# A clock model in the planner, spare products in planned gaps, and a new order of preference for a two-layer kernel

## The chip, the core and the metric

The kernel runs on one core of a Trainium2 chip. A core has a matrix engine (TensorE, PE in the profile, with its weight loads as PEld), a vector engine (VectorE, DVE), a scalar engine (ScalarE, ACT), a general engine (GpSimd, POOL) and a queue engine that issues DMAs (SyncE, SP). The metric is the device time of one launch in microseconds, the median over several runs. The profile is one execution taken by the hardware profiler; its span runs from the first to the last instruction.

## The reference

The input x is 8 sequences of 512 tokens with 256 channels, in float32. Two layers follow each other; after each of the four blocks comes x = layernorm(x + block(x)).

1. **Retention.** q, k, v = x W_qkv, 16 heads of 16 channels. ret = (q k^T) with a causal decay per head; r = ret v + (q past_kv) x 256; then a normalization over a whole sequence (mean and variance of all heads, tokens and channels), with a weight and a bias per head.
2. **Feed-forward with ternary weights.** W_fc (1024 x 256) and W_proj (256 x 1024) are quantized to -1, 0, 1 by thresholds at half of their mean magnitude. h = layernorm(gelu(x W_fc^T)), then the product with W_proj.
3. **Attention within a token.** An RMS norm, q, k, v for 16 heads of 16 channels, elu on q and k, and for each token a product over its heads, in two halves whose difference is taken with a factor lambda; RMS norms over a head and over the token; then two 256 x 256 products with a gelu between, and a residual.
4. **Routed experts.** Tokens in 2 groups of 2048, a router to 8 experts, two per token, at most 160 tokens per expert and group. Each expert computes relu(x wi) wo with 1024 hidden channels; results are summed with the gates.

## The kernel before

All work is cut into stages, one per sequence b (batch) or expert i, each written as a Python generator. `stage_a1` is retention (transposes of x, projections, then four chunks of 128 tokens: scores `sc`, masking into `scm`, values `r_ps`, a running state). `stage_a2` is its normalization and residual (two tiny products `gn_ps`, `gn_ps2`, then transposes `r_tp`). `stage_b` is the feed-forward (transposes, `fc_ps`, gelu and squares, `pr_ps`). `stage_bn` is the layer norm behind it, on VectorE, GpSimd and ScalarE alone. `stage_c1` is the attention of block 3 (transposes of x, `qk_ps`, `v_ps`, then per chunk `v_tp`, `hs`, masking into `hm`, `at_ps`). `stage_c2` is all behind that: the RMS norms on VectorE, transposes of a, the products `w1_ps` and `w2_ps`, the layer norm, its stores (`x3_d`, `y_d`), and the router's logits. `choose` and `route` select experts and build the lists of rows. `gather`, `dispatch`, `expert_in`, `expert_out` and `combine` do the experts, and `finish` the last layer norm. `prepare_ffn` and `prepare_l1` quantize or transpose the weights once.

The order of instructions on every engine is made by a planner when the program is built. `op` places an operation off TensorE on a model of its engine, with a cost in us, and puts it into a list by planned start; `pe(cost)` advances the planned time of TensorE, `Plan.now`. A stage yields when it would wait: `need(t)` for data and a free PSUM bank, `hold` for a buffer, `later` for time alone. `bank` hands out one of eight PSUM banks, the one released first, and `release` gives it back at a planned time. `interleave` (L250) holds a list of streams. Each turn it asks every stream when its next stage could go on, and takes the earliest; TensorE work can't go before `Plan.now`, so several streams often have equal times, and then the one that stands first in the list wins:

```python
                if on_pe:
                    t = max(t, Plan.now)
                if best is None or t < best[0]:
                    best = t, i
```

Each engine executes its instructions in the order that results, waiting where a semaphore says so. The planner's costs thus decide only the order; what a wait really takes is decided on the chip. Lists of streams stand at the end of `tile_layers`: weights of the experts first, then loads of x, `c2`, `bn`, `c1`, gathers, dispatches, routing, `a2`, weights' preparation, `a1`, `b`, and the experts' stages.

PSUM results are moved off by ACT or DVE. In the profile nearly all instructions off TensorE carry line L204, since `op` issues them; they are told apart by the names of their tiles. A float32 product shows as two MATMUL rows, a transpose or a product in the rounded float32 format of `fc_ps` as one.

Of the kernel before, what the change touches and what calls it, by code (L numbers as in the profile page):

```python
# [21 lines left out]
B, S, D = 8, 512, 256  # L22
# [59 lines left out]
def tile_layers(ctx: ExitStack, tc: tile.TileContext, ins, out, at):  # L82
# [64 lines left out]

    class Plan:
        now = 0.0
        t = 0.0  # L150
        events = []
        count = 0
# [62 lines left out]

    def pe(cost):

        Plan.now = Plan.t = max(Plan.now, Plan.t) + cost
        return Plan.now + PE_OUT

    def bank(name):
# [28 lines left out]
    def interleave(streams):  # L250

        ends = {}
        queues = [list(q) for q in streams]
        at, kind = [0.0] * len(streams), ["other"] * len(streams)
        begun = [False] * len(streams)  # L260
        clock = 0.0
        first = {"a1", "b", "c1", "h", "e", "s", "d"}
        while any(queues):
            best = None
            for i, q in enumerate(queues):
                if not q:
                    continue
                key, deps, takes, _ = q[0]
                t = max(at[i], clock)
                on_pe = kind[i] == "pe"  # L270
                if not begun[i]:
                    if any(k not in ends for k in deps):
                        continue
                    if any(len(Plan.free[k]) < n for k, n in takes.items()):
                        continue
                    on_pe = key[0] in first
                    t = max([t] + [ends[k] + (HOP_PE if on_pe else 0.0) for k in deps])
                    t = max([t] + [sorted(Plan.free[k])[n - 1] for k, n in takes.items()])
                if on_pe:
                    t = max(t, Plan.now)  # L280
                if best is None or t < best[0]:
                    best = t, i
            t, i = best
            key, _, takes, gen = queues[i][0]
            if not begun[i]:
                begun[i] = True
                for k, n in takes.items():
                    take(k, n)
            clock = Plan.t = t
            flush(t)  # L290
            try:
                kind[i], at[i] = next(gen)
            except StopIteration as stop:
                ends[key] = max(t, stop.value or 0.0)
                queues[i].pop(0)
                begun[i], kind[i], at[i] = False, "other", t
        flush(HELD)
# [254 lines left out]
    with ExitStack() as stages:  # L552
# [253 lines left out]
        def load_x(b):  # L806
            if b > 0:
                fetch_x(b)
            t = Plan.t + (5.0 if b == 0 else 22.0 if b == 1 else 6.0)
            yield later(t)  # L810
            return t
# [177 lines left out]
        def stage_a2(b):  # L989

            rT, st, ready = rTs.pop(b)
            x_sb = xs[b]
            mv = wk.tile([P, 2], F32, tag="gn_mv", name=f"gn_mv_{b}")
            gs = wk.tile([P, 3], F32, tag="gn_s", name=f"gn_s_{b}")
            t = op(DVE, 0.26, ready, V.bn_aggr, mv, st)
            yield from need(t)
            ps = bank("gn_ps")
            T.matmul(ps[:, 0:1], ones, mv[:, 0:1], start=True, stop=True)

            def spread():  # L1000
                nc.vector.tensor_tensor(gs[:, 1:2], mv[:, 0:1], gs[:, 0:1], ALU.add)
                nc.vector.scalar_tensor_tensor(
                    gs[:, 1:2], gs[:, 1:2], gs[:, 1:2], mv[:, 1:2], ALU.mult, ALU.add
                )

            t = op(
                DVE, 0.15, pe(0.2), V.tensor_scalar, gs[:, 0:1], ps[:, 0:1], -1.0 / P, None, ALU.mult,
                bank=ps,
            )
            t = op(DVS, 0.42, t, spread)  # L1010
            yield from need(t)
            ps = bank("gn_ps2")
            T.matmul(ps[:, 0:1], ones, gs[:, 1:2], start=True, stop=True)
            t = rsqrt(gs[:, 2:3], ps[:, 0:1], 1.0 / P, LN_EPS, pe(0.2), bank=ps)

            ga = wk.tile([P, 2, 2], F32, tag="gn_a", name=f"gn_a_{b}")

            def affine():
                nc.vector.tensor_scalar(ga[:, 0, :], gnp[:, 0, :], gs[:, 2:3], None, ALU.mult)
                nc.vector.scalar_tensor_tensor(  # L1020
                    ga[:, 1, :], ga[:, 0, :], gs[:, 0:1], gnp[:, 1, :], ALU.mult, ALU.add
                )

            t = op(DVS, 0.48, t, affine)
            e1 = op(
                ACT, 0.81, t, A.activation, rT[:, 0, :], rT[:, 0, :], AF.Identity,
                bias=ga[:, 1, 0:1], scale=ga[:, 0, 0:1],
            )
            e2 = op(
                POOL, 0.76, t, GP.tensor_scalar, rT[:, 1, :], rT[:, 1, :], ga[:, 0, 1:2],  # L1030
                ga[:, 1, 1:2], ALU.mult, ALU.add,
            )
            r = x_sb
            ts = []
            for c2 in range(NC // 2):
                yield from need(max(e1, e2))
                ps = bank("r_tp")
                for c in range(2):
                    for m in range(2):
                        at_ = (c * 2 + m) * P  # L1040
                        c4 = c2 * 2 + c
                        T.transpose(ps[:, at_ : at_ + P], rT[:, m, c4 * P : (c4 + 1) * P], ident)
                e = op(
                    DVE, 0.68, pe(0.46), V.tensor_tensor,
                    r[:, c2 * 2 : c2 * 2 + 2, :].rearrange("p c d -> p (c d)"), ps,
                    x_sb[:, c2 * 2 : c2 * 2 + 2, :].rearrange("p c d -> p (c d)"), ALU.add, bank=ps,
                )
                ts += [e, e]
            give("aq", Plan.now)
            ends = layernorm(wk, r, r, ts, on_act=True)[3]  # L1050
            x1s[b] = r
            yield later(max(ends))
            return max(ends)
# [334 lines left out]
        def open_experts(k):  # L1388

            (ret_stack, ffn_stack)[k].close()  # L1390
            pools[k] = stages.enter_context(
                tc.tile_pool(name=f"mo{k}", bufs=1, side=("left", "right")[k], reuse_waits="tile")
            )
            yield later(Plan.t)
            return Plan.t
# [42 lines left out]
        def dispatch(g, pair):  # L1438

            rows, tag = gathered.pop((g, pair))  # L1440
            xsT[g, pair] = pools[0].tile(
                [P, NK, 2 * CAP], F32, tag="xsT", bufs=2, name=f"xsT_{g}_{pair}"
            )
            for k in range(NK):
                yield from need(0.0)
                ps = bank("xs_tp")
                for j, n in enumerate(COLS):
                    T.transpose(
                        ps[:, j * P : j * P + n], rows[:n, j, k * P : (k + 1) * P], ident[:n, :n]
                    )  # L1450
                done = op(
                    ACT, 0.43, pe(0.57), A.copy, xsT[g, pair][:, k, :], ps[:, : 2 * CAP], bank=ps
                )
            give(tag, Plan.now)
            yield later(done)
            return done
# [111 lines left out]
        def after(*keys):  # L1568
            return [k for k in keys if k[1] >= 0 and (k[0] != "p" or k[1] < 2)]
# [9 lines left out]
                for i in range(n)  # L1579
            ],  # L1580
            [(("x", b), after(("x", b - 1), ("a1", b - 2)), {"x": 1}, load_x(b)) for b in range(B)],
            [(("c2", b), after(("c1", b)), {"m4": 2}, stage_c2(b)) for b in range(B)],
            [(("bn", b), after(("b", b)), {}, stage_bn(b)) for b in range(B)],
            [
# [5 lines left out]
                for g in range(G) for pair in (range(NE2), reversed(range(NE2)))[g]  # L1590
            ],
            [
                (("d", g, pair), [("g", g, pair), ("o", 1)], {"xsT": 1}, dispatch(g, pair))
                for g in range(G) for pair in (range(NE2), reversed(range(NE2)))[g]
            ],
# [2 lines left out]
                    (("t", b), [("c2", b)], {}, choose(b, wk))  # L1598
                    for b in range(g * half, (g + 1) * half)
                ] + [(("r", g), [], {"m4": 2}, route(g, wk))]  # L1600
            ],
            [(("a2", b), after(("a1", b)), {}, stage_a2(b)) for b in range(B)]
            + [(("o", 0), [], {}, open_experts(0))],
            [
                (("p", 0), [], {"b8": 2}, prepare_ffn()),
                (("p", 1), [], {"m4": 1}, prepare_l1()),
            ],
            [
                (("a1", b), after(("x", b), ("b", b - 3), ("p", b - 1)), {"aq": 3, "T": 1}, stage_a1(b))
                for b in range(B)  # L1610
            ],
            [
                (("b", b), after(("a2", b), ("p", 0), ("c1", b - 2)), {"T": 2}, stage_b(b))
# [53 lines left out]
```

## Time and profile before

| | |
|---|---|
| median of 3 runs | 976.57 us (976.17 to 978.56) |
| profiled execution | 982.84 us |
| its span | 981.1 us |
| TensorE busy (products) | 879.1 us, 7516 rows |
| VectorE, ScalarE, GpSimd busy | 602.1, 453.2, 393.8 us |
| mean granted TensorE clock | 0.948 |
| last product ends | 950.1 us after the span's start |

The profile page divides the span into 40 slices of 24.5 us. Its digits are the busy share of each engine in tenths, and the row PEclk is the clock that the throttle granted to TensorE, in tenths of full speed. A query for stretches gives busy times between any two moments, with the mean granted clock; one for the order of time lists the rows of an engine, equal neighbours merged, with the idle time before them in brackets and what ended it. "Who waited for whom" adds such idle times up by pair: total us, times, longest. All times in such answers count from the span's start.

### The profile page before, as it was taken

The page shows a single profiled execution, that of the slowest core. Times are in us where ns is not written, and L with a number is a line of the kernel's source. Part 1 is how long each engine was busy: PE and PEld are TensorE (multiplying, and loading weights), DVE is VectorE, ACT ScalarE, POOL GpSimd, SP SyncE. Part 2 cuts the span into 40 slices and gives each one's busy share as a digit, 9 for nine tenths or more (in the row PEclk, how much of TensorE's full clock was granted, in tenths as well). Part 3 has the DMA queues.
Part 4 walks back from the last instruction along what each step waited for, and adds up shares of the span by engine and source line. Part 5 has one row for each costly group of instructions (what it writes and reads, how often), then busy time and mean ns, then how long its engine had stood idle before and what let it go on. Part 6 is the DMA issues. An engine that isn't in the chain of part 4 may idle for free. (4 is left out here: it accounts for less than half of the span.)

```text
span 981.1 us, 18435 instructions
## 1 busy us (share of the span) xinstructions
PE 879.1 (90%) x7516; PEld 687.0 (70%) x7516; DVE 602.1 (61%) x1485; ACT 453.2 (46%) x866; POOL 393.8 (40%) x395
## 2 busy tenths in 40 slices
PE   7799999998969899999999989968979999999870
PEld 4668767766747677766867766755657889899860
DVE  2954466579656768686786788676865743502213
ACT  2346367264524584278268427726635342122213
POOL 3336336152344355326345525514454231353331
PEclk9999999998879999999999989998989999999985
DMA  6020000001001000100010001031104176239635
GB/s 205 28 87 2 0 2 2 1 22 44 1 22 44 1 2 1 47 20 2 1 65 2 1 1 44 2 139 47 58 0 156 46 219 192 63 96 346 189 84 176
DMA packets 49652, 60.34 MB, mean 62 GB/s; under 512 B 5536, under 2 KB 44960, under 8 KB 49568
## 3 DMA queue, kind: packets, MB, share of 16 engines
q1 hardware_dynamic: 45600, 53.92, 16.4%
q0 software_dynamic: 3968, 5.25, 3.0%
q8 instruction: 59, 0.97, 0.4%
q14 instruction: 25, 0.20, 0.1%
HBM read 43.43 MB, written 15.73 MB: 60 GB/s over the span
## 5 line engine op out<-in xcount | busy, mean ns | idle before, releaser
L1108 PE MATMUL pr_ps<-prT,fT 128*128 128x257 f32 x512 | 122.0, 392 | 1.2 <-DVE scm L204 0.7
L1108 PEld LDWEIGHTS pr_ps<-prT,fT 128*128 128x128 f32 x512 | 98.6, 196 | 17.8 <-DVE scm L204 1.1
L204 POOL TENSOR_TENSOR fsq<-fsq,fsf 128x512 f32<-128x512 f32 x56 | 72.4, 1292 | 41.7 <-ACT fsf L204 39.4
L1471 PE MATMUL wi_ps<-xsT,wi 128*128 128x160 f32 x512 | 78.6, 308 | 0.0
L204 POOL DMA_INDIRECT y_d<-eo,srci x24 | 37.3, 1554 | 98.1 <-ACT eo L204 45.8
L1471 PEld LDWEIGHTS wi_ps<-xsT,wi 128*128 128x128 f32 x512 | 74.1, 197 | 0.6 <-issue 0.2
L1500 PE MATMUL wo_ps<-e_hT,wo 128*128 128x160 f32 x512 | 74.2, 300 | 0.0
L204 DVE TENSOR_TENSOR hm<-hs,cst 128x512 f32<-128x512 f32 x96 | 60.0, 677 | 20.0 <-PE hs L1247 18.3
L1500 PEld LDWEIGHTS wo_ps<-e_hT,wo 128*128 128x128 f32 x512 | 70.7, 190 | 1.0 <-issue 0.6
L204 ACT ACTIVATE e_hT<-wi_ps 128x480 f32<-128x480 f32 (+1 forms) x48 | 25.2, 527 | 97.4 <-PE wi_ps L1471 97.4
L204 POOL TENSOR_TENSOR ln_rs<-ln_rs,mhalf 128x4 f32<-128x4 f32 x32 | 34.5, 1077 | 86.9 <-DVE ln_rs L204 86.8
L204 DVE TENSOR_TENSOR scm<-sc,cst 128x512 f32<-128x512 f32 x96 | 60.7, 678 | 9.3 <-PE sc L911 9.1
L1188 PE MATMUL qk_ps<-l1T,x2T 128*128 128x512 f32 x128 | 63.1, 616 | 0.0
L204 POOL TENSOR_TENSOR scm<-scm,cst 128x512 f32<-128x512 f32 x32 | 42.6, 1330 | 50.4 <-ACT scm L204 41.5
L204 POOL TENSOR_TENSOR hm<-hm,cst 128x512 f32<-128x512 f32 x32 | 40.9, 1278 | 52.1 <-ACT hm L204 52.0
L204 DVE STREAM_TRANSPOSE hT<-pad 128x512 f32<-128x512 f32 x64 | 59.3, 959 | 2.4 <-ACT pad L204 1.9
L863 PE MATMUL qk_ps<-xT,wqkv 128*128 128x512 f32 x128 | 60.1, 617 | 0.0
L1079 PE MATMUL fc_ps<-x1T_l,fcT 128*128 128x512 f32 x128 | 53.9, 421 | 0.3 <-ACT scm L204 0.3
L1079 PE MATMUL fc_ps<-x1T_h,fcT 128*128 128x512 f32 x128 | 50.3, 393 | 0.0
L204 ACT ACT_TABLE_LOAD x37 | 47.5, 1283 | 1.5 <-PEq L1653 0.7
L204 POOL TENSOR_SCALAR pad<-pad,lamv 128x128 f32<-128x128 f32 x32 | 12.0, 375 | 88.2 <-DVE pad L204 87.6
L1247 PE MATMUL hs<-hT 16*128 16x128 f32 x1024 | 40.6, 289 | 4.0 <-DVE scm L204 4.0
(238 smaller groups left out, 1933.9 us busy)
## 6 DMA issues: line engine op xcount, KB each, us to landing
wi<-in_L_ffn_wi SPq DMA_DIRECT2D x13, 1024.0 KB, 8.4
wo<-in_L_ffn_wo SPq DMA_DIRECT2D x13, 1024.0 KB, 6.4
x<-in_L_attn_x SPq DMA_DIRECT2D x8, 512.0 KB, 4.2
x_d<-a SPq DMA_DIRECT2D x8, 512.0 KB, 3.0
y_d<-a SPq DMA_DIRECT2D x8, 512.0 KB, 4.4
z<-y_d SPq DMA_DIRECT2D x8, 512.0 KB, 4.4
out<-z SPq DMA_DIRECT2D x8, 512.0 KB, 3.0
prepare<-in_L_ffn_W_fc SPq DMA_DIRECT2D x1, 1024.0 KB, 12.0
```

The costliest lines, as they stand in the source:

```text
L204: heapq.heappush(Plan.events, (t, Plan.count, lambda: fn(*args, **kw)))
L863: T.matmul(ps, wqkv[:, k, which * D + m * P : which * D + (m + 1) * P], xT[:, k, :], start=(k == 0), stop=(k == NK - 1),)
L1079: T.matmul(ps, fcT[:, k, f * P : (f + 1) * P], x[:, k, :], start=(k == 0 and x is low), stop=(k == NK - 1 and x is high),)
L1108: T.matmul(acc[:, : D + 1], hT[:, f, c * P : (c + 1) * P], prT[:, f, :], start=(f == 0), stop=(f == NF - 1),)
L1188: T.matmul(qk, x2T[:, k, cs], l1T[:, k, 0:2, :].rearrange("p a d -> p (a d)"), start=(k == 0), stop=(k == NK - 1),)
L1247: T.matmul(sc[r][:, g * P : (g + 1) * P], hT[rows, g, P : 2 * P], hT[rows, g, :P], start=True, stop=True,)
L1471: T.matmul(ps[:, f * CAP : (f + 1) * CAP], wi[:, k, (f3 + f) * P : (f3 + f + 1) * P], x[:, k, es], start=(k == 0), stop=(k == NK - 1),)
L1500: T.matmul(ps[:, m * CAP : (m + 1) * CAP], wo[:, f, m * P : (m + 1) * P], hT[:, f, :], start=(f == 0), stop=(f == NF - 1),)
```

## The change

Three things change, all in the planner.

`pe` gets a model of TensorE's clock: if the planned idle time before a product is over 1.5 us, products are counted at up to twice their cost until 1.5 us after the gap's end, or 8 us after it where the gap was 3 us or longer.

`interleave`, when the earliest candidate is TensorE work that starts over 1.4 us after `Plan.now`, and a bank is free by then, takes a bank named `spare` and issues products of a constant with the identity matrix into it, 128 x 256, one for each 0.44 us, until the gap left is 0.9 us or less. Their results are not read.

In the list of streams, `a2` and the preparation of weights move from behind routing to behind the loads of x; `a1` moves to ahead of the dispatches; so routing comes behind both.

```diff
     class Plan:
         now = 0.0
+        slow = 0.0
         t = 0.0
...
     def pe(cost):
-        Plan.now = Plan.t = max(Plan.now, Plan.t) + cost
+        start = max(Plan.now, Plan.t)
+        if start - Plan.now > 1.5:
+            Plan.slow = start + (1.5 if start - Plan.now < 3.0 else 8.0)
+        cost += min(max(Plan.slow - start, 0.0) / 2, cost)
+        Plan.now = Plan.t = start + cost
         return Plan.now + PE_OUT
...
                 if best is None or t < best[0]:
-                    best = t, i
-            t, i = best
+                    best = t, i, on_pe
+            t, i, on_pe = best
+            if on_pe and t - Plan.now > 1.4 and Plan.now > 0.0 and min(Plan.banks) <= Plan.now:
+                ps = bank("spare")
+                while t - Plan.now > 0.9:
+                    T.matmul(ps[:, :256], ident, cst[:, :256], start=True, stop=True)
+                    Plan.now += 0.44
+                release(ps, Plan.now)
             key, _, takes, gen = queues[i][0]
...
             [(("x", b), after(("x", b - 1), ("a1", b - 2)), {"x": 1}, load_x(b)) for b in range(B)],
+            [(("a2", b), after(("a1", b)), {}, stage_a2(b)) for b in range(B)]
+            + [(("o", 0), [], {}, open_experts(0))],
+            [
+                (("p", 0), [], {"b8": 2}, prepare_ffn()),
+                (("p", 1), [], {"m4": 1}, prepare_l1()),
+            ],
             [(("c2", b), after(("c1", b)), {"m4": 2}, stage_c2(b)) for b in range(B)],
...
+            [
+                (("a1", b), after(("x", b), ("b", b - 3), ("p", b - 1)), {"aq": 3, "T": 1}, stage_a1(b))
+                for b in range(B)
+            ],
             [
                 (("d", g, pair), [("g", g, pair), ("o", 1)], {"xsT": 1}, dispatch(g, pair))
...
                 ] + [(("r", g), [], {"m4": 2}, route(g, wk))]
             ],
-            [(("a2", b), after(("a1", b)), {}, stage_a2(b)) for b in range(B)]
-            + [(("o", 0), [], {}, open_experts(0))],
-            [
-                (("p", 0), [], {"b8": 2}, prepare_ffn()),
-                (("p", 1), [], {"m4": 1}, prepare_l1()),
-            ],
-            [
-                (("a1", b), after(("x", b), ("b", b - 3), ("p", b - 1)), {"aq": 3, "T": 1}, stage_a1(b))
-                for b in range(B)
-            ],
```

Since the planner places each instruction by its planned times, the order changes on all engines from the first chunk on. Apart from the 80 spare products (160 rows) and four table loads fewer on ScalarE, the instructions are the same.

## The prediction

> **What bounds the kernel now.** First the page: where TensorE is busy, slice by slice, and at which clock.
>
> ```profile
> span 981.1 us, 18435 instructions
> ...
> PE 879.1 (90%) x7516; PEld 687.0 (70%) x7516; DVE 602.1 (61%) x1485; ACT 453.2 (46%) x866; POOL 393.8 (40%) x395
> ...
> PE   7799999998969899999999989968979999999870
> ...
> PEclk9999999998879999999999989998989999999985
> ```
>
> TensorE is the bound until its last product at 950.1 us; then 31 us of scatter, reload and last layer norm follow, which the change leaves alone. Up to 950.1 it is idle 950.1 - 879.1 = 71 us, and the clock row dips just after the busy row does. Next, stretches of the span (busy us and count for PE, PEld, DVE, ACT, POOL; then granted clock, DMA share, GB/s):
>
> ```profile
> 54.00:650.00 596.00, 563.04 (x5052) 419.48 (x5049) 412.99 (x1004) 318.35 (x596) 260.20 (x268) 0.97 0.05 17
> 650.00:755.00 105.00, 85.41 (x575) 61.24 (x576) 72.85 (x190) 52.45 (x100) 47.78 (x44) 0.89 0.25 86
> 755.00:950.00 195.00, 188.21 (x1549) 174.59 (x1547) 76.32 (x205) 58.75 (x126) 61.82 (x52) 0.98 0.52 157
> ```
>
> Third, TensorE's rows in order of time round two long gaps (start, us, what; in brackets the gap before and who ended it):
>
> ```profile
> 650.09 3.73 PE L1108 MATMUL pr_ps<-prT,fT 128*128 128x257 f32 x16
> 653.66 1.03 PE L1042 MATMUL r_tp<-cst_ident,q 128*128 128x128 f32 x8
> 664.91 2.80 PE L335 MATMUL tp<-cst_ident,x 128*128 128x128 f32 x8 [10.22 <-ACT x L204]
> ```
>
> ```profile
> 732.49 1.97 PE L335 MATMUL tp<-cst_ident,a 128*128 128x128 f32 x8 [7.00 <-DVE a L204]
> 734.25 5.66 PE L1108 MATMUL pr_ps<-prT,fT 128*128 128x257 f32 x16
> ```
>
> Eight transposes take 1.03 us warm, 1.97 after the gap; sixteen rows (eight products, two rows each) 3.73 against 5.66, partly recovered. So a gap is paid twice: idle, then half clock. The granted clock shows 13 half-clock stretches inside the work (eight of 3.4 us, one of 6.8, four of 10.2), 75 us in all; TensorE was busy for 57 of them, so 57/2 = 28.5 us are lost. Thus 950.1 = 850.7 work at full clock + 70.9 idle + 28.5 clock. Last, who is waited for:
>
> ```profile
> PE tp L335 <- DVE a L204: 21.8, 4, 8.5
> PE tp L335 <- ACT x L204: 15.4, 9, 10.2
> PE eo_tp L1533 <- DVE eoT L204: 6.6, 3, 3.9
> ```
>
> The first is stage_c2's norm chain (last at_ps of a batch, to transposes of a); the second stage_bn's layer norm (last pr_ps, to stage_c1's transposes). Their seven gaps: 2.4, 8.5, 3.9, 7.0 and 2.0, 2.2, 10.2 = 36.2 us. The 10.2 is a queue, as DVE's rows there show: c2's two multiplies for batch 5 stand ahead of batch 6's statistics.
>
> ```profile
> 659.17 1.23 DVE L204 TENSOR_TENSOR a<-ap,hs 128x1024 f32<-128x1024 f32 x1
> 660.43 1.22 DVE L204 TENSOR_TENSOR a<-a,g2b 128x1024 f32<-128x1024 f32 x1
> 661.57 0.42 DVE L347 BATCH_NORM_STATS2 ln_st<-x 128x6 f32<-128x256 f32 x1
> ```
>
> **Spare products.** The built order holds 80, in 16 groups: 6+5+5+7 in batch 0's retention, 57 later (11 before batch 0's transposes of a; 3+4+3+8 round stage_c1 of batch 6; the rest 2 to 6). None is in the trace. Nearest row: L1108, eight products of 257 columns, spaced 0.43 us (3.73 less the last one's drain). So 80 x 0.43 = 34.6 us: 9.9 at the start, 24.6 later (unrounded spacing). Below: 0 if all lie in real gaps; above: 34.6. I count all as work and let the gaps shrink instead. They are products, not transposes, so they should count as activity. They read constants and write a bank that the plan holds free; a wait on one costs 0 to 1 us, I take 0.
>
> **The rule.** The Trainium skill, "TensorE: Matmul & The Clock Gate" (the clock gate, and its closing table), says half clock follows an idle window of about 3.4 us and asks only that no gap exceed about 3 us. By it the groups of 2 to 4 (27 spares, 11.7 us) are waste. The trace differs: gaps of 1.4, 1.5, 2.0, 2.1, 2.4 each had a 3.4 us half-clock stretch after them, 24 of the 75 us stand behind gaps under 3, though 1.1, 1.2 and one of 2.2 had none. A 3.4 us stretch costs up to 1.7, as four spares do. By the rule spares gain some 5 us less; I go by the rows.
>
> **The new order.** The clock in the plan's costs issues nothing; it and the moved streams only reorder. Off TensorE nothing is added or removed but four of 37 table loads on ACT (1.28 us each, behind other work there). I compare each chain's latency before with the TensorE work that the new order puts between its ends (each product at its own full-clock spacing: 0.86 for 512 columns, 0.43 for 256, 0.27 for 160, 0.11 a transpose; spares included).
> - stage_bn: latency 6.4 and 7.1 where it stalled cleanly, about 7 elsewhere. Work before: 4.8, 12.9, 5.0, 6.3, 9.3, 10.8, 0.9, 8.1 for batches 0 to 7; after: 9.5, 14.0, 9.3, 15.5, 8.0, 14.0, 5.9, 9.8. In DVE's new order the c2 multiplies no longer stand before batch 6's statistics. Left: about 1 (batch 6).
> - stage_c2: latency 17.7, 21.5, 20.7, 17.9, under 29, 21.5, 23.5, 16.5. Work before: 15.9, 13.1, 17.1, 17.9, 23.6, 8.6, 16.4, 16.7; after: 19.8, 20.0, 22.2, 22.2, 28.1, 19.2, 19.6, 16.4. Left: 1.5 (1), 2.3 (5), about 2 (6, at 21.5: the 23.5 held cold time). Together some 8 instead of 36.2.
> - Routing: between its last product and the first dispatch of group 0 stand 106 us (99 before): hidden. For group 1, 9.8 against 12.5; POOL issues three row gathers there, 1.0 each plus 0.3, and with sources and landing about 8.5: hidden by a little; without that cover 1 to 3.
> - SP's queue: batch 5's two stores move ahead of the first expert weights (hidden, some 190 us early); batch 7's two behind expert 6's load, which waits for expert 3 to finish: some 5 us late, needed only by group 1's gathers some 25 us on. Batch 2's input load moves ahead of one weight: hidden.
>
> **The start**, walked by hand. DVE now puts the reduction of W_fc (2.28) between two maskings of chunk 0 (0.65 each), so that chunk's values end near 26.7 instead of 24.1; then thresholds (0.4), two ternary passes (1.53, 2.35) and the second reduction (2.28) stand ahead of chunk 1's masking: 34.7, values 36.5 (28.9 before). Weights are ready sooner, but pr_mean's subtraction (2.3) now stands ahead of chunk 3's masking: it starts near 55.4, batch 0 ends at 58.9 against 54.0. Loss 4.9, between 0 and 8.
>
> **The sum.** Idle before 54.0 was 11.6, clock loss 1.7. Work after it: 896.1 - 59.3 - 26.9 = 810 (896.1 = 950.1 - 54.0). Idle after: chains 8, last stage 6.6 (2.1, 3.9, 0.6, order there nearly unchanged), gaps under 0.4 us 4.2, others 10 (12.2 before, scattered; a new order is about as likely to make such) = 29. Clock: some six stretches of 3.4 left, at 1.7 each: 10 (26.9 before). 58.9 + 810 + 24.6 + 29 + 10 = 932.5, so 17.6 less than 950.1. The profiled execution took 982.84 (span 981.1 and 1.7 round it), the median 976.57; 17.6 off the latter gives 959.
>
> **Rivals.**
> 1. Faster still, 944: the start costs nothing (5 off), incidental gaps halve (5), clock loss 5: 17.6 + 15 = 32.6. For: most work now exceeds its latency. Against: the walk at the start.
> 2. Spares don't hold the clock, 969: they leave holes, or count too little; 10 more of loss. For: the gate's phase decides (2.2 without, 1.4 with half clock). Against: products at full clock all around.
> 3. The waits come back in VectorE's queue. For batch 5 choosing experts now stands inside c2's chain, for 1 and 6 a layer norm's statistics. If all bn and c2 latencies grow by x, the stalls go from 7 to 21 at x = 2.3, with 0.3 us of clock per us: the 17.6 is gone. At 3.5 they are 33: 26 x 1.3 = 33.5 more, hence slower, 992. Against: DVE is busy 61%, and the chain of 10.2 has lost its obstacle.
>
> **From cases to numbers.** Forecast 0.55 (own range 950 to 968), rival 1 0.13, rival 2 0.12, rival 3 0.20, of which 0.08 ends within 0.3% (about what can be told from no change) and 0.12 slower. Faster 0.80, same 0.08, slower 0.12. For 8 in 10 the range leaves out half of rival 1's cases and the slower ones: 943 to 978.
>
> **What would show it.** Right: the gaps before batch 6's and 7's transposes shrink from 10.2 and 7.0 to under 3; granted clock over 0.96 in the stretch of stage_c1 and c2 of batch 6 (0.89); half-clock time in the work from 75 to under 35 us; PE busy about 895; batch 0's retention ends near 59. Wrong: c2 or bn latencies 2 us longer, a clock that dips behind spares, new waits of TensorE on masked scores, or a start beyond 62.

## The result, and the profile after

The changed kernel takes 963.64 us (median of 4 runs, 958.6 to 966.18) against 977.22 for the kernel before (4 runs): a ratio of 0.9854, 95% interval 0.9812 to 0.9896. It is faster by 1.5%; the forecast was 959, within 943 to 978. The profiled execution took 966.18 us, 16.7 less than the one before.

The page of the changed kernel, with TensorE's busy time, its digits by slice, and the granted clock:

```profile
span 964.4 us, 18726 instructions
...
PE 896.7 (93%) x7676; PEld 703.8 (73%) x7676; DVE 608.7 (63%) x1485; ACT 445.2 (46%) x862; POOL 393.9 (41%) x395
...
PE   7999999999999998999997999979999999999860
...
PEclk9999999999999999999999899989999999999895
```

TensorE has 160 rows more and is busy 17.6 us longer, yet ends earlier: its last product ends at 933.6 us, not at 950.1. Ahead of the last product's slice, the 39th, four holes are left in the busy row: a 7 in the 22nd slice and in the 27th, an 8 in the 16th and in the 38th. The clock row dips in the 23rd, the 27th and the 38th slice, in or just behind three of them.

By stretches of the changed kernel (columns: busy us and count of PE, PEld, DVE, ACT, POOL; granted clock, DMA share, GB/s):

```profile
54.00:370.00 316.00, 311.39 (x2778) 233.67 (x2777) 210.43 (x513) 175.26 (x332) 150.61 (x157) 0.99 0.06 20
370.00:650.00 280.00, 261.15 (x2309) 194.32 (x2308) 218.62 (x504) 140.34 (x272) 114.77 (x116) 0.97 0.05 16
650.00:755.00 105.00, 102.71 (x871) 77.75 (x871) 73.86 (x195) 55.93 (x106) 47.52 (x47) 1.00 0.31 104
```

From 650 to 755 us TensorE is busy for 102.7 of 105 us, at full clock; before it was 85.4, at 0.89. The middle went the other way: for the same stretch from 370 to 650 us the kernel before had 268.9 us busy at 0.98, against 261.2 at 0.97 here (the two orders do not do the same work in a stretch).

Who waits for whom, TensorE's largest rows in the changed kernel (us in total, times, longest):

```profile
PE tp L348 <- DVE a L205: 9.9, 5, 5.7
PE inv_ps L530 <- DVE route L205: 5.9, 1, 5.9
```

The waits for `a` of stage_c2 fell from 21.8 to 9.9 us, those for `x` behind stage_bn's layer norm from 15.4 to some tenths. A wait of 5.9 us for routing is new.

For the experiments one sum is used throughout, taken from the trace's rows: the end of TensorE's last product = work at full clock + idle + clock loss, where the loss is half of the time that TensorE was busy inside half-clock stretches before that end.

| kernel | last product ends | work | idle | half-clock time | clock loss |
|---|---|---|---|---|---|
| before | 950.1 | 850.6 | 71.0 | 75.1 | 28.5 |
| changed | 933.6 | 885.0 | 36.9 | 27.3 | 11.7 |

The spares bring 34.4 us of work, the change as a whole takes away 34.1 of idle and 16.8 of clock loss: 16.5 us earlier.

### The profile page after: what moved, and what is told of

It is laid out like the page before. It is cut to its first block, busy times and chain, and to the rows that moved or that the text cites. A ratio compares the mean times of both kernels' runs of the same rounds, so it can differ in the third digit from the quotient of the medians.

```text
span 964.4 us, 18726 instructions
## 1 busy us (share of the span) xinstructions
PE 896.7 (93%) x7676; PEld 703.8 (73%) x7676; DVE 608.7 (63%) x1485; ACT 445.2 (46%) x862; POOL 393.9 (41%) x395
## 3 DMA queue, kind: packets, MB, share of 16 engines
q1 hardware_dynamic: 45600, 53.92, 16.7%
## 4 chain that ended last, share of the span: by engine, by line
PE 66%; DVE 19%; ACT 6%; POOL 4%; issue 3%; DMA 2%; POOLq 0%; ACTq 0%; SPq 0%; DVEq 0%
PE wi_ps L1484 7%; PE wo_ps L1513 7%; PE pr_ps L1121 6%; PE qk_ps L1201 4%; PE fc_ps L1092 4%; PE qk_ps L876 4%; PE hs L1260 3%; PE w_ps L1354 3%; PE tp L348 3%; PE r_ps L957 3%; PE at_ps L1275 2%; DVE a L205 2%; PE w_ps L1343 2%; PE sc L924 2%; PE v_ps L1207 2%
## 5 line engine op out<-in xcount | busy, mean ns | idle before, releaser
L1121 PE MATMUL pr_ps<-prT,fT 128*128 128x257 f32 x512 | 117.2, 382 | 0.3 <-ACT scm L205 0.3
L1121 PEld LDWEIGHTS pr_ps<-prT,fT 128*128 128x128 f32 x512 | 95.5, 189 | 16.6 <-issue 1.9
L205 POOL TENSOR_TENSOR fsq<-fsq,fsf 128x512 f32<-128x512 f32 x56 | 72.6, 1296 | 30.2 <-ACT fsf L205 27.6
L205 POOL DMA_INDIRECT y_d<-eo,srci x24 | 37.2, 1549 | 81.1 <-ACT eo L205 42.9
L205 POOL TENSOR_TENSOR hm<-hm,cst 128x512 f32<-128x512 f32 x32 | 40.9, 1279 | 48.3 <-ACT hm L205 48.3
L205 ACT ACTIVATE x<-x,ln_nb,ln_rs 128x256 f32<-128x256 f32 x64 | 33.2, 590 | 31.2 <-DVE ln_nb L205 31.2
L205 DVE COPY eoT<-wo_ps 128x320 f32<-128x320 f32 x16 | 7.8, 489 | 60.0 <-PE wo_ps L1513 60.0
```

What stands on the lines that cost most here:

```text
L205: heapq.heappush(Plan.events, (t, Plan.count, lambda: fn(*args, **kw)))
L1121: T.matmul(acc[:, : D + 1], hT[:, f, c * P : (c + 1) * P], prT[:, f, :], start=(f == 0), stop=(f == NF - 1),)
```

## The experiments

The prediction gave one sum for the whole change. The runs take its two halves apart: the filling of gaps, and the new order that comes with the model of the clock and the list of streams. Ratios are against the kernel before, run on the same chip.

### Are the spare products worth their time?

**The same order without spares (e1_no_spares).** The plan advances as if they were there; they are not issued. Spares aside, the order on every engine is that of the changed kernel.

```diff
-                ps = bank("spare")
+                spare = Plan.banks.index(min(Plan.banks))
                 while t - Plan.now > 0.9:
-                    T.matmul(ps[:, :256], ident, cst[:, :256], start=True, stop=True)
                     Plan.now += 0.44
-                release(ps, Plan.now)
+                Plan.banks[spare] = Plan.now
```

> The changed kernel in its own order, without the 80 spare products (its planner counts them, but none is issued). Theory (a gap is paid twice, spares lie mostly in real gaps and hold the clock): 35 us of TensorE work go, but in the changed kernel's trace all but some 6 us of them stand where the next product's data was late anyway, so idle rises by about 29, and each opened gap of 1.3 to 5 us brings 3.4 or 10 us of half clock: clock loss from 12 to about 30. 963.6 - 6 + 18 = about 976, between 970 and 982; half-clock time in the work about 70 us instead of 27. Rival (the order alone brings the gain, spares are a cost): 930 to 958, half-clock time about the same.

Measured: 967.31 us, ratio 0.988 (0.9852 to 0.9909). Its page, TensorE's rows:

```profile
PE 873.8 (91%) x7516; PEld 682.7 (71%) x7516; DVE 606.9 (63%) x1485; ACT 446.6 (46%) x862; POOL 394.0 (41%) x395
...
PE   6899999969999999899899789978899999999960
...
PEclk9799999989999999899999899988899999999995
```

The busy row has its holes back and the clock row its dips, and still the last product ends at 933.8 us, 0.2 later than with spares. The sum says why: work 850.5, idle 60.0, clock loss 23.3. The 80 spares cost 34.5 us, of which 23.1 lay in real gaps and 11.4 outside them, and they save 11.6 of clock loss. That is nothing on balance. The expectation for this run was too high: it put only 6 us of the spares outside real gaps, and the clock loss without them at 30.

One place of each kind. TensorE's rows in the order of time, first of the changed kernel, then without spares (start, us, what; in brackets the idle time before and who ended it):

```profile
203.94 0.66 PE L1078 MATMUL tp<-cst_ident,x 128*128 128x128 f32 x4 [1.89 <-DVE scm L205]
204.65 6.70 PE L294 MATMUL spare<-cst,cst_ident 128*128 128x256 f32 x22
211.19 1.04 PE L348 MATMUL tp<-cst_ident,a 128*128 128x128 f32 x8
...
665.10 0.33 PE L1387 MATMUL lg_tp<-cst_ident,lgT 128*128 128x128 f32 x1
665.26 1.46 PE L294 MATMUL spare<-cst,cst_ident 128*128 128x256 f32 x6
666.93 0.38 PE L1011 MATMUL gn_ps<-gn_mv,cst 128*128 128x1 f32 x2 [0.21 <-DVE gn_mv L205]
667.18 1.97 PE L294 MATMUL spare<-cst,cst_ident 128*128 128x256 f32 x8
668.99 0.54 PE L348 MATMUL tp<-cst_ident,x 128*128 128x128 f32 x3
```

```profile
207.41 0.66 PE L1077 MATMUL tp<-cst_ident,x 128*128 128x128 f32 x4 [1.90 <-DVE scm L205]
213.64 1.97 PE L347 MATMUL tp<-cst_ident,a 128*128 128x128 f32 x8 [5.58 <-DVE a L205]
...
667.63 0.33 PE L1386 MATMUL lg_tp<-cst_ident,lgT 128*128 128x128 f32 x1
669.57 0.35 PE L1010 MATMUL gn_ps<-gn_mv,cst 128*128 128x1 f32 x2 [1.61 <-DVE gn_mv L205]
670.76 1.95 PE L347 MATMUL tp<-cst_ident,x 128*128 128x128 f32 x4 [0.84 <-ACT x L205]
```

At 204.65 eleven spares stand in a gap of 5.58 us, and the transposes behind them take 1.04 us instead of 1.97. But the spares take 6.70 themselves, as 3.4 us of them ran at half clock: the 1.89 us gap ahead of them, which the plan did not foresee, had already turned it down. At 665 three and four spares stand in gaps of 1.61 and 0.84, and the transposes of x start 3.89 us after `lg_tp` with them, 3.13 without: the spares are longer than the gaps.

**Only the wide gaps filled (e5_wide_gaps).** The bookkeeping stays for all groups, products are issued only where the planned gap is over 3 us: 38 spares in 5 groups.

```diff
-                ps = bank("spare")
+                spare = Plan.banks.index(min(Plan.banks))
+                ps = bank("spare") if t - Plan.now > 3.0 else None
                 while t - Plan.now > 0.9:
-                    T.matmul(ps[:, :256], ident, cst[:, :256], start=True, stop=True)
+                    if ps is not None:
+                        T.matmul(ps[:, :256], ident, cst[:, :256], start=True, stop=True)
                     Plan.now += 0.44
-                release(ps, Plan.now)
+                if ps is not None:
+                    release(ps, Plan.now)
+                Plan.banks[spare] = Plan.now
```

> The changed kernel's order with spares issued only where the planned gap is over 3.0 us: 5 groups, 38 products, 16.4 us of work. By the page's rule (only gaps over about 3 us matter): all of the clock's hold is kept and 18 us of work go, 946 to 955 here, half-clock time near 27 us. By the rows (each gap of 1.4 us and more costs a half-clock stretch): the eleven groups left out open their gaps, half-clock time 42 to 52 us, and the last product ends near 934 as with all and with none: ratio 0.984 to 0.990.

Measured: 963.93 us, 0.9863 (0.9832 to 0.9893); last product at 929.3, with work 866.2, idle 46.6, loss 16.5. Half-clock time is 41.0 us, close to what was expected by the rows (42 to 52), and the 946 to 955 us expected by the page's rule did not come. Against the run without spares these 38 cost 15.7 us of work and give back 13.4 idle and 6.8 clock. In the profiled executions that is 4.5 us earlier; the ratios of the three kernels do not tell them apart.

**Spares twice as wide (e6_double).** 512 columns each, everything else the same.

```diff
-                    T.matmul(ps[:, :256], ident, cst[:, :256], start=True, stop=True)
+                    T.matmul(ps, ident, cst[:, :512], start=True, stop=True)
```

> The changed kernel's order with each spare product twice as wide (128 x 512, two rows of 0.43 us): 34.5 us more work in the same 16 places. If all of it lies on the path that sets the end, ratio 0.985 + 0.036 = 1.021; the gaps left behind spares (3.0, 1.1, 0.5 and less, some 6 us) and what clock loss they still bring can take some, so 1.012 to 1.021. Rival (other engines' chains set the end for long stretches, not TensorE): under 1.005.

Measured: 987.47 us, 1.0099 (1.0068 to 1.0129), slower than the kernel before, if a little less so than expected. Work rises by 29.1 us, idle falls by 4.8 and loss by 3.2, and the last product ends 21.2 later, at 954.8. So with one width the gaps are about full, and of what is added three quarters lie on the path.

**Wide gaps filled in another order (e10_clock_wide).** This uses the order of e7 below (clock model and new list), which it leaves as it is: the spares don't advance the plan.

```diff
+            if on_pe and t - Plan.now > 3.0 and Plan.now > 0.0 and min(Plan.banks) <= Plan.now:
+                spare, free = Plan.banks.index(min(Plan.banks)), min(Plan.banks)
+                ps = bank("spare")
+                for _ in range(int((t - Plan.now - 0.9) / 0.44)):
+                    T.matmul(ps[:, :256], ident, cst[:, :256], start=True, stop=True)
+                release(ps, free)
```

> The order of the clock model with the new list (0.9651), exactly kept, and 33 spare products (14.3 us of work) issued in its four planned gaps of over 3 us, without the planner counting them. If spares are worth nothing net, as in the changed kernel's order with all and with none (933.6 and 933.8), the last product ends at 908 to 913 as without them (910.8), ratio 0.961 to 0.968: idle 48 to about 36, clock loss 12 to about 8. If wide gaps are worth filling (in the changed kernel's order the five wide ones gave an end at 929.3): 905 to 908, ratio 0.957 to 0.963.

Measured: 945.48 us, 0.966 (0.9622 to 0.9699), against 0.9651 for the same order without them. The 33 spares add 13.7 us of work and remove 11.2 of idle; the clock loss is 11.8 in both, and the last product ends at 913.2 us against 910.8. In two orders, then, spares are worth nothing that can be measured.

### Products or transposes?

**Transposes as spares (e4_transposes).** The Trainium skill, "TensorE: Matmul & The Clock Gate" (Part 4, on transposes in TensorE's own mode), says that these do not count as busy in the same way and that full clock does not come on for them; the prediction used this as a reason why spare products should count. Four transposes fill the time of one product.

```diff
-                    T.matmul(ps[:, :256], ident, cst[:, :256], start=True, stop=True)
+                    for n in range(4):
+                        T.transpose(ps[:, n * P : (n + 1) * P], cst[:, n * P : (n + 1) * P], ident)
```

> The changed kernel with four 128x128 transposes in the place of each spare product, about the same 0.43 us. Theory (any work of TensorE holds the clock): within 4 us of the changed kernel's 963.6, half-clock time 25 to 40 us. Rival (the Trainium skill's page on TensorE has it that transposes do not count as busy for the clock): half clock behind every group of them, as in the kernel without spares, and the same work: 978 to 988, half-clock time 70 us or more.

Measured: 965.79 us, 0.9837 (0.9793 to 0.988). The rows at the place shown above, with transposes:

```profile
204.16 0.66 PE L1079 MATMUL tp<-cst_ident,x 128*128 128x128 f32 x4 [1.89 <-DVE scm L205]
204.88 6.69 PE L295 MATMUL spare<-cst_ident,cst 128*128 128x128 f32 x44
211.40 1.04 PE L349 MATMUL tp<-cst_ident,a 128*128 128x128 f32 x8
```

Forty-four transposes take 6.69 us where eleven products took 6.70, and the transposes of a behind them run at full clock in the same 1.04. Half-clock time is 27.3 us in both kernels, at the same places. Here float32 transposes of 128x128 held the clock as products do; the measurement decides against the page.

### Which part of the order brings the gain?

| kernel | clock model | new list | spares | ratio | work | idle | clock loss |
|---|---|---|---|---|---|---|---|
| before | - | - | - | 1 | 850.6 | 71.0 | 28.5 |
| e3 | - | yes | - | 1.0007 (0.9994 to 1.0021) | 855.8 | 66.9 | 25.8 |
| e9 | yes | - | - | 1.0105 (1.0062 to 1.0149) | 855.8 | 74.0 | 29.0 |
| e7 | yes | yes | - | 0.9651 (0.9624 to 0.9677) | 850.6 | 48.3 | 11.8 |
| e8 | - | yes | 96 | 0.9946 (0.9924 to 0.9968) | 896.3 | 36.8 | 7.8 |
| e2 | yes | - | 123 | 0.9876 (0.9849 to 0.9902) | 904.5 | 27.6 | 1.7 |
| changed | yes | yes | 80 | 0.9854 (0.9812 to 0.9896) | 885.0 | 36.9 | 11.7 |

Spares alone were not run. The kernels e3 and e9, which have no spares, show 5 us more work than the kernel before; why is not known.

**The new list alone (e3_streams_only)**, in the kernel before; **the old list in the changed kernel (e2_old_streams)**. Both edits are the moves of the list, in e2 backwards; the first line of one move:

```diff
+            [(("a2", b), after(("a1", b)), {}, stage_a2(b)) for b in range(B)]
...
-            [(("a2", b), after(("a1", b)), {}, stage_a2(b)) for b in range(B)]
```

> The new list of streams alone: no clock model, no spares. Theory (the spares' hold on the clock brings the gain): gaps and half clock stay as before, 968 to 985, clock loss above 20 us. Rival (the order brings the gain): 955 to 966.

> Clock model and spare products with the list of streams as before. The planner now plants 118 spares, 51 us of work. Theory (spares are free in real gaps and hold the clock): the order is worse by its larger gaps, but the clock holds: 38 more spares are 16 us of gaps that the new list did not have, so about 980, between 968 and 988, granted clock as in the changed kernel. Rival (only spares matter, the list does not): 960 to 966.

Measured: 980.72 us, no change, for the first; 967.13 us for the second, as fast as with the new list, and just between its two expectations (968 and more, 966 and less). The kernel with the old list has nearly rid itself of half clock (3.4 us in all) and holds its idle time to 27.6, the second least of all runs. Yet its 123 spares cost 54 us of work, which eats most of what they save.

**Everything but the clock model (e8_no_clock_model).**

```diff
-        start = max(Plan.now, Plan.t)
-        if start - Plan.now > 1.5:
-            Plan.slow = start + (1.5 if start - Plan.now < 3.0 else 8.0)
-        cost += min(max(Plan.slow - start, 0.0) / 2, cost)
-        Plan.now = Plan.t = start + cost
+        Plan.now = Plan.t = max(Plan.now, Plan.t) + cost
```

> Spare products and new list, no clock model: 86 spares, 37 us, in other places. Theory A (the clock model makes the order, spares are worth nothing net): as the list alone, ratio 0.996 to 1.006; spares' 37 us are taken from idle and clock loss in equal amount. Rival B (filling makes the order): 0.980 to 0.990.

Measured: 973.25 us, 0.9946, between its two expectations; 96 spares were issued, not 86. **The clock model and the new list, no spares (e7_clock_streams)**: the block that issues them is deleted, and with it the advance of the plan.

```diff
-            if on_pe and t - Plan.now > 1.4 and Plan.now > 0.0 and min(Plan.banks) <= Plan.now:
-                ps = bank("spare")
-                while t - Plan.now > 0.9:
-                    T.matmul(ps[:, :256], ident, cst[:, :256], start=True, stop=True)
-                    Plan.now += 0.44
-                release(ps, Plan.now)
```

> Clock model and new list of streams, no spare products and no filling of planned gaps (so a gap also slows the planned products behind it). The runs so far: without its spares, in the same order, the changed kernel's last product ends at 933.8 us as with them (933.6), and the new list alone gives nothing (1.0007). Theory A (the clock model in the plan makes the better order): ratio to before 0.980 to 0.992, idle of TensorE near 60 us, clock loss near 23. Rival B (the filling of gaps in the plan makes the order): 0.996 to 1.004, idle 65 or more, loss 25 or more.

Measured: 944.01 us, 3.5% below the kernel before and well below the changed one. Neither expectation had this. It was tempting to say that the clock model makes the good order. Three further runs tested that against the rival that each of these orders is a draw from a wide scatter.

**The clock model alone (e9_clock_only)**: the same deletion, with the old list. **The changed kernel and e7, with one constant moved by 0.01 us (e11_after_nudged, e12_clock_nudged)**: `PE_OUT`, the time that the plan puts between a product's end and its result. The edit of both:

```diff
-    PE_OUT = 0.14
+    PE_OUT = 0.15
```

> The clock model in the planner alone: list of streams as before, no filling, no spare products. With the new list it gave 0.9651 to before. Theory A (the clock model makes the better order, the list matters little, as the list alone gave 1.0007): 0.960 to 0.980. Rival C (model and list are needed together, or the good order is luck): 0.985 or more.

> The changed kernel with one cost of the planner nudged by 0.01 us (a product's way out of TensorE, 0.15 for 0.14): same rules, other ties, 64 spares instead of 80; the order is the same up to product 1659 of 4244. Theory A (filling and spares make a worse order than the clock model alone): 0.975 to 0.992, near the changed kernel's 0.985. Rival L (orders scatter by chance by 20 us and more, so that differences of this size between planner's rules show little): anything from 0.955 to 1.01.

> The clock model with the new list and no filling, nudged by the same 0.01 us; the order is the same up to product 610 of 4244. Theory A: 0.958 to 0.975, near 0.9651. Rival L: as for the other nudged kernel, with no tie to which rule it has.

Measured: e9 takes 989.5 us, 1.0105, slower than before, as rival C allowed. A row of its order of time shows one place that costs it:

```profile
461.74 1.94 PE L341 MATMUL tp<-cst_ident,a 128*128 128x128 f32 x8 [11.97 <-DVE a L205]
```

e9 and e7 have the same order for the first 797 of 4244 products; then the list decides ties otherwise, and this order ran into a gap of 12 us that the other does not have.

e11 takes 943.01 us, 0.9639 (0.9601 to 0.9677), outside theory A's range. Its page and its wait for the norm of stage_c2:

```profile
span 941.9 us, 18688 instructions
...
PE   7999999999999999899999999999999999999960
...
PEclk9999999999999999999999999999999999999995
```

```profile
PE tp L348 <- DVE a L205: 2.1, 2, 1.5
PE inv_ps L530 <- DVE route L205: 1.7, 1, 1.7
```

The order is that of the changed kernel for the first 1659 products, and spares, model and list are the same. A hundredth of a microsecond in the plan thus moved the time by 2.2%, more than the whole change did. The waits for `a` went from 9.9 to 2.1 us and that for routing from 5.9 to 1.7; idle is 25.8, clock loss 8.5, and 64 spares are issued instead of 80. e12 takes 945.94 us, 0.9673 (0.9636 to 0.9711): the same nudge left e7's gain nearly as it was.

So the gain of the changed kernel lies in its order, but no one rule of the change can be credited with it. The list by itself gave nothing and the model by itself a loss; together they gave 3.5%, and with the spares' bookkeeping in the plan 1.5% or 3.6%, as a hundredth falls. Of the four orders made with model and list, three (e7, whose order e10 shares, e11 and e12) lie near 0.965 and that of the changed kernel at 0.985; the five made without the one or the other lie between 0.9876 and 1.0105. That may point to something systematic in the two together, but with two nudges it is not shown, and stays open.

## Why the prediction was right

**The end of TensorE's work** was forecast at 932.5 and measured at 933.6. Its terms hold in total: work 850.7 + 34.6 = 885.3 against 885.0; idle 37.3 (8.3 up to the end of batch 0's retention and 29 after it) against 36.9 (6.6 and 30.2); clock loss 10 against 11.7, but as two half-clock stretches of 3.4 us and three of 6.8, where six of 3.4 were put. The 31 us behind TensorE stayed 30.8. TensorE is busy 896.7 (about 895), half clock fell to 27.3 us (under 35) and the clock from 650 to 755 us is 1.00 (over 0.96).

**The start.** Batch 0's retention ends at 57.8, forecast 58.9, before 54.0: the walk through VectorE's queue was right to about a microsecond.

**The chains.** The gaps of 10.2 and 7.0 before batch 6's and 7's transposes are gone, as forecast, and the stalls behind stage_bn and stage_c2 sum to 10.2 us where 8 were put. They are not where the forecast put them. Batches 1 and 6 of c2 have 0 and 0.2 us of stall instead of 1.5 and 2, batch 2 has 3.0 instead of none, and batch 5 has 5.7 instead of 2.3.

The step that was mis-sized is the latency, taken over from the kernel before. Where TensorE waited for it, stage_c2's chain took 24.5, 22.7, 37.2 and 28.5 us for batches 2 to 5, against 20.7, 17.9, under 29 and 21.5 before. That is one of the signs that the prediction named for being wrong, at four of eight batches. It cost only 9.7 us of stalls: for batches 2 and 3 some 22 us of TensorE work stood in the stretch, as forecast, and in batch 4's stretch, the longest, lies the routing gap of 5.9 us. That the sum of the stalls came near the forecast is thus partly luck.

For batch 5 the rows show where the 7.0 us come from. Before, the transpose of the attention's result, the sum `hss` that the norm needs, and the four products `t` late in the chain:

```profile
649.99 0.72 DVE L204 STREAM_TRANSPOSE ap<-at_ps 128x512 f32<-128x512 f32 x1 [0.80 <-PE at_ps L1262]
651.83 1.22 DVE L204 TENSOR_REDUCE hss<-t 128x64 f32<-128x1024 f32 x1
665.42 1.67 DVE L204 SCALAR_TENSOR_TENSOR t<-g3b,rms_ss,a 128x256 f32<-128x256 f32 x4
```

The same three in the changed kernel, and below them rows of ScalarE and one of GpSimd:

```profile
608.99 0.70 DVE L205 STREAM_TRANSPOSE ap<-at_ps 128x512 f32<-128x512 f32 x1
615.50 1.22 DVE L205 TENSOR_REDUCE hss<-t 128x64 f32<-128x1024 f32 x1 [0.20 <-ACT t L205]
627.49 5.70 DVE L205 SCALAR_TENSOR_TENSOR t<-g3b,rms_ss,a 128x256 f32<-128x256 f32 x4 [1.13 <-POOL rms_ss L205]
```

```profile
609.63 1.28 ACT L205 ACT_TABLE_LOAD   x1
610.93 0.23 ACT L205 ACTIVATE choose<-logits 128x32 f32<-128x32 f32 x1
611.17 1.28 ACT L205 ACT_TABLE_LOAD   x1
...
614.41 1.06 ACT L205 ACTIVATE t<-ap 128x1024 f32<-128x1024 f32 x1
...
627.42 5.47 POOL L205 TENSOR_TENSOR fsq<-fsq,fsf 128x512 f32<-128x512 f32 x4
```

From the transpose to `hss` it is 6.5 us instead of 1.8. VectorE chooses experts in between (609.62 to 613.7), but what comes last is the square `t` on ScalarE, which stands behind the exponential of that choice, its two table loads and rows of the feed-forward until 614.4. So choosing does stand in the chain, as rival 3 said, but it holds ScalarE's queue more than VectorE's. Later the four products `t` take 5.70 us instead of 1.67, while GpSimd multiplies `fsq`. These two add 8.7 us, and the rest of the chain ran 1.7 shorter. In e11, at the same place, `hss` starts 2.4 us after the transpose, GpSimd does no such product beside `t`, the chain takes 16.3 us, and TensorE does not wait:

```profile
635.26 1.67 DVE L205 SCALAR_TENSOR_TENSOR t<-g3b,rms_ss,a 128x256 f32<-128x256 f32 x4
```

What batch 5's chain costs TensorE in the changed kernel is this:

```profile
628.49 0.44 PE L931 MATMUL kd_tp<-cst_ident,kT 128*128 128x128 f32 x2
634.59 1.94 PE L348 MATMUL tp<-cst_ident,a 128*128 128x128 f32 x8 [5.67 <-DVE a L205]
636.32 3.27 PE L294 MATMUL spare<-cst,cst_ident 128*128 128x256 f32 x8
```

The four spares stand behind the gap, not in it, because the plan had its gap there; at half clock they take 3.27 us, and the gap stays unfilled.

**The other gaps.** The routing gap of 5.9 us, before `inv_ps`, was not foreseen as such; it is part of the 12.7 us that came where 10 were put for "others".

**From the trace to the median.** The profiled execution fell by 16.7 us, forecast 17.6. Taken off the median of 976.57 that gives 959.9, and 963.64 was measured: the profiled execution of the kernel before lay 6.3 us above its median, that of the changed one only 2.5 above its own. Most of the 4.6 us between forecast and result is this.

**The rule on gaps.** The prediction weighed the Trainium skill's limit of some 3 us for a gap against the rows, and went by the rows. The runs bear that out for what follows a short gap: without spares, gaps of 1.76, 1.91, 1.98 and 2.67 us in the first 60 us each had a half-clock stretch of 3.4 us behind them. They do not bear out the use made of it. A spare group in such a gap costs as much as it saves. The rows do show windows of 3.4 us, but one need not be idle to be followed by half clock: what counts is how busy TensorE is in it (last section). So before the change, the gap of 2.2 us that had no half clock behind it fell across two windows, in which TensorE was busy for 52 and 69%; the one of 1.4 fell into a window busy for 54%, where both outcomes occur.

**What was right for the wrong reason.** The sum did not ask what the spares earn by themselves: it took their 34.6 us as work and the fall of idle and clock loss as one thing. Rival 2 asked only whether spares hold the clock; they do, and pay for it in full.

## What to carry to other kernels

A product that only keeps the clock up is work on the path: count how much of it lies in gaps that really occur, and half of the half-clock time that it prevents, and issue it only if that sum exceeds its cost; here 80 of them came out at zero. A latency read from an old order holds only while the same rows stand beside it on the other engines: one chain here grew from 21.5 to 28.5 us by a queue on ScalarE and a product on GpSimd. Where a planner decides the order, first nudge one of its constants by a hundredth: if that alone moves the time by 2%, a single run of any change to the planner says little about its rules, and several nudged builds of each version are the comparison to make. Here that search gave versions at 0.964 to 0.967 of the time before, better than the change itself.

## What the runs showed of the hardware

Transposes as filler held TensorE's clock as float32 products did: half clock for 27.3 us in both kernels, at the same places.

Gaps far below 3 us can be followed by half clock: behind one of 1.89 us in the changed kernel the clock was halved from 205.6 to 209.0, while behind its gap of 1.13 at 31.3 it was not. The rows of clock and TensorE show what decides. In each of the 14 traces all changes of the granted clock lie a whole multiple of 3.413 us apart. The full-clock time up to the last product, cut into windows of this length, gives this for the half clock in the next window:

| TensorE busy in the window | windows | half clock in the next |
|---|---|---|
| under 45% | 71 | 71 |
| 45 to 73% | 88 | 23 |
| over 73% | 3462 | 0 |

So a gap counts by what it leaves of one window, together with its neighbours: the window up to 205.6 us was busy for 47%. Products issued after such a window do not end the half clock early: the eleven spares at 204.65 ran through the 3.4 us at half clock, 1.9 us longer than they take at full clock.

VectorE's product `t` (128x256, float32) took 0.45 to 0.48 us 25 times in the changed kernel and 1.48 to 1.49 seven times; each of the seven ran while GpSimd multiplied two tiles of 128x512 (`fsq` or `scm`), none of the 25 did.
